# Moving a division by three key blocks, stores to another queue, and a normalisation into pairs, in a fused attention block

## The chip, the cores and the metric

The kernel runs on one core of one Trainium2 chip. The metric is the time of the core for one execution, in microseconds (us), as the median over several executions. A run is called slow when it is more than 1.5% above the fastest of its kernel.

## The reference, cut to what matters

```python
# x: (16, 512, 32, 32) float32; 8 groups, 4 heads of 128, n = 32 * 32 = 1024 positions
xn   = group_norm(x) * gamma + beta
q, k, v = split(einsum('oc,bchw->bohw', qkv_w, xn) + qkv_b)
attn = softmax(einsum('bhnd,bhmd->bhnm', q, k) * 128 ** -0.5)
out  = einsum('bhnm,bhmd->bhnd', attn, v)
return x + einsum('oc,bchw->bohw', proj_w, out) + proj_b
```

## The kernel before

It works through 16 batches of 4 heads of 8 key blocks. In each key block TensorE makes scores (s), ScalarE their exponential (p), VectorE adds p to a running sum (tot), and TensorE adds to the weighted sum (po). Between these, units of the big products are spread over the heads: q and k of heads 2 and 3 of the batch in head 0, the projection of the batch before in head 1, q and k of heads 0 and 1 of the next batch in head 2, v of the next batch in head 3. The big products use two levels of Strassen's scheme. Their weights, with the sums of weights worked out once, are kept in DRAM and loaded in groups into two buffers.

```python
wpool = ctx.enter_context(tc.tile_pool(name="w", bufs=2))

def group_weights(site, g, first):
    group = OUTER[g]                          # ((1, 5), (2, 6), (7, 4), (3,))
    w = wpool.tile([P, 2, 7, P], F32, tag="w", name=f"w_{site}_{g}")
    if not first:
        nc.sync.dma_start(w[:, : len(group)], store[site, g])     # 896 KB, or 448
        return w
    # ... first use: build the sums, keep them
```

So the third group of weights can be loaded only when the last product of the first group has read its buffer.

The inner sums of the activations are kept too, for the second pair of heads:

```python
def inner_sum(m):
    # ... a, c: the two terms of t1, t2, t3 or t4
    for i in range(n):
        nc.vector.tensor_sub(have[m][:, i, :], inner(i, a), inner(i, c))
    if sums == "keep":
        t = dpool.tile([P, n, Q], F32, tag=f"{m}_{g}", bufs=1, name=f"kept_{m}_{g}")
        inner_kept[b, g, m] = t
        nc.sync.dma_start(t, have[m][:, :n])
```

A head's output is divided by its sums of exponentials in the head that follows. The reciprocals take a round through DRAM:

```python
def denominators(b, h):
    # ... sums of tot over the partitions, reciprocal r
    nc.sync.dma_start(row.rearrange("o (c i) -> (o c) i", i=BLK), r)
    nc.sync.dma_start(rinv[b, h], row.to_broadcast((P, N)))

def divide(b, h):
    nc.vector.tensor_mul(os_[b, h], os_[b, h], rinv.pop((b, h)))

for s in range(steps + 1):
    # ... j: key block, units: what plan_head puts into this block
    for half in range(NH2):
        if s < steps:
            scores(s, half)
            if half == 0 and j == 2 and s > NB:
                divide(*where(s - NB)[:2])
        if s > 0:
            weighted_sum(s - 1, half)
        run(units[half * n : (half + 1) * n])
```

A scheduler orders each engine's queue when the kernel is built: it has a model of when inputs are there, and the place in the source decides only between candidates.

Names in the profile: w is a buffer of weights and kept its store in DRAM; xt is a sum of blocks of x, qk_t an inner sum (of parts of one block or block sum) and kept_t its copy in DRAM; qk_x and qk_y (the "y bank") hold TensorE's products for q and k until VectorE or ScalarE has emptied them, into qk_r among others; row and rinv are the reciprocals on their round through DRAM; vd and v are v on its way through DRAM.

## Time and profile before

| | before |
|---|---|
| time, median (range, runs) | 3326.03 us (3324.56 to 3336.82, 4) |
| span of the profiled run | 3336.0 us |
| TensorE busy | 3218.4 us (96%) |
| TensorE waits for the y bank behind the division | 69.2 us, 15 times |
| TensorE waits for weights (w<-kept) | 9.7 us, 17 times |

The lines behind these numbers stand in the prediction. In a line of waits the three numbers are the sum in us, how often, and the longest. In a line of the timeline they are the start and the length in us, then engine, source line, operation, output<-input; in brackets the idle time before it and what ended it. A line of the chain (the work that ended last) has start, length and transfer. A line of DMA issues ends with the size of one and the median us from issue to landing.

The profiled run is the slowest of the four, 11 us over their median, so some of its idle time may be that run's own.

One more table is worked out from the trace and not a view of the page. In this trace matmul instructions of 512 columns that follow each other without a break start 0.429 us apart, those of 256 columns 0.215 us. For each instruction I take the time from its start to the next one's start, less 0.4267 us for 512 columns and in proportion for fewer, and call the rest **idle time**: waits, what a lowered clock costs, and the 2 or 3 ns by which the amount taken off is too small (some 17 us). The work taken off is the same 3095 us in all kernels here, so a difference in span is a difference in idle time. A head begins with the last s of the head before, so that a gap just ahead of its own first s is its own; what follows the very last s is put in head 0:

| idle us, 15 batches | batch 0 | head 0 | head 1 | head 2 | head 3 | sum |
|---|---|---|---|---|---|---|
| before | 22.1 | 135.7 | 26.3 | 31.7 | 7.9 | 223.7 |

Head 0 holds the wait behind the division and the slower clock that goes with it.

### The profile page before, as it was taken

Reading aid. Unit: us, or ns where it says so; the run is one execution under the profiler, and the core shown is the slowest. Engines: PE = TensorE matmul, PEld = TensorE weight load, DVE = VectorE, ACT = ScalarE, POOL = GpSimd, SP = SyncE. Lnnn points to the kernel's source line nnn. Section 1 sums busy time; section 2 is a strip of 40 time slices with the busy share of each in tenths; the row PEclk is TensorE's granted clock in tenths of the full one; section 3 lists DMA queues with packets and bytes.
Section 4 is the critical chain, followed back from the end, with each engine's and each line's share of the span. In section 5 each row is a group of like instructions: output and inputs, shape, how many; then the busy total and the mean of one; then the engine's idle time right before and its main releaser. Section 6 shows DMA issues by size and latency. Waiting matters only on the chain.

```text
span 3336.0 us, 33513 instructions
## 1 busy us (share of the span) xinstructions
PE 3218.4 (96%) x10474; PEld 2187.3 (66%) x10474; DVE 2522.8 (76%) x4161; ACT 1440.8 (43%) x2709; POOL 387.4 (12%) x682
## 2 busy tenths in 40 slices
PE   8999999999999999999999999999999999999999
PEld 6566666666666666666666666666666666666664
DVE  7876868768687686877878677786777867778675
ACT  2534435344353443534435354353534535344342
POOL 0001021010211102011020100202002020020100
PEclk9999999999999999999999999999999999999999
DMA  6665564555645557454564645646456464564731
GB/s 222 213 207 176 171 212 142 183 173 180 204 160 177 169 171 217 154 185 154 186 203 157 196 146 178 207 152 201 149 172 216 152 203 151 168 206 161 221 127 45
DMA packets 227958, 589.27 MB, mean 177 GB/s; under 512 B 32960, under 2 KB 72384, under 8 KB 227776
## 3 DMA queue, kind: packets, MB, share of 16 engines
q1 hardware_dynamic: 176944, 427.63, 39.2%
q0 software_dynamic: 48960, 157.33, 15.0%
q10 hardware_dynamic: 1872, 2.11, 0.2%
q8 instruction: 86, 1.41, 0.2%
q14 instruction: 96, 0.79, 0.1%
HBM read 448.28 MB, written 138.67 MB: 176 GB/s over the span
## 4 chain that ended last, share of the span: by engine, by line
PE 66%; DVE 16%; DMA 10%; issue 6%; POOL 1%; ACT 0%; SPq 0%; POOLq 0%; DVEq 0%; ACTq 0%
PE po L796 18%; PE s L711 18%; PE qk_x L509 7%; PE qk_y L509 6%; PE v_x L509 5%; PE pp_x L509 4%; PE v_y L509 4%; PE pp_y L509 3%; DMA w<-kept 3%; DMA rinv<-row 2%; DMA row<-r 2%; DVE qk_t L494 2%; DVE tot L724 1%; DMA y<-in_x 1%; DVE vt L648 1%
## 5 line engine op out<-in xcount | busy, mean ns | idle before, releaser
L716 ACT ACTIVATE p<-s 128x512 f32<-128x512 f32 x1024 | 610.5, 596 | 1058.6 <-PE s L711 1051.8
L711 PE MATMUL s<-qk,qk 128*128 128x512 f32 x2048 | 1059.5, 599 | 2.7 <-ACT p L716 2.4
L796 PE MATMUL po<-p,v 128*128 128x512 f32 x2048 | 1059.6, 599 | 0.9 <-ACT o L803 0.9
L796 PEld LDWEIGHTS po<-p,v 128*128 128x128 f32 x2048 | 603.4, 303 | 335.5 <-issue 218.0
L724 DVE TENSOR_TENSOR tot<-tot,p 128x1024 f32<-128x1024 f32 x385 | 469.4, 1219 | 108.0 <-ACT p L716 105.0
L711 PEld LDWEIGHTS s<-qk,qk 128*128 128x128 f32 x2048 | 391.7, 192 | 98.4 <-issue 33.5
L509 PE MATMUL qk_x<-qk_t,w 128*128 128x256 f32 x1344 | 363.4, 387 | 8.4 <-ACT qk_u L420 6.5
L509 PEld LDWEIGHTS qk_x<-qk_t,w 128*128 128x128 f32 x1344 | 249.5, 192 | 183.9 <-issue 67.0
L528 DVE TENSOR_TENSOR qk_r<-qk_y,qk_u 128x512 f32<-128x512 f32 (+1 forms) x256 | 158.6, 619 | 159.6 <-ACT qk_u L420 134.6
L420 ACT COPY qk_u<-qk_x 128x512 f32<-128x512 f32 (+1 forms) x256 | 136.4, 533 | 261.1 <-PE qk_x L509 261.1
L659 POOL DMA_DIRECT2D vd<-vu x120 | 66.4, 553 | 1376.6 <-DVE vu L651 1350.9
L509 PE MATMUL qk_y<-qk_t,w 128*128 128x256 f32 x448 | 132.9, 412 | 69.1 <-DVE qk_r L528 68.9
L806 DVE TENSOR_TENSOR o<-o,rinv 128x1024 f32<-128x1024 f32 x63 | 77.1, 1225 | 144.2 <-DMA rinv<-row 143.7
L509 PE MATMUL pp_x<-pp_t,w_proj 128*128 128x256 f32 x630 | 173.3, 389 | 0.0
L509 PEld LDWEIGHTS v_x<-v_t,w_v 128*128 128x128 f32 x630 | 118.4, 190 | 79.1 <-issue 38.3
L509 PE MATMUL v_x<-v_t,w_v 128*128 128x256 f32 x630 | 166.6, 381 | 0.0
L528 DVE TENSOR_TENSOR v_r<-v_y,v_u 128x512 f32<-128x512 f32 (+1 forms) x120 | 74.6, 622 | 121.4 <-ACT v_u L420 113.6
L509 PEld LDWEIGHTS pp_x<-pp_t,w_proj 128*128 128x128 f32 x630 | 113.9, 190 | 63.7 <-issue 18.9
L664 POOL DMA_DIRECT2D v<-vd x240 | 139.8, 590 | 98.1 <-DMA vd<-vu 45.2
L509 PEld LDWEIGHTS qk_y<-qk_t,w 128*128 128x128 f32 x448 | 89.6, 204 | 92.1 <-DVE qk_r L528 74.5
L509 PE MATMUL qk_y<-x,w 128*128 128x256 f32 x512 | 145.7, 382 | 2.2 <-DVE x L272 2.1
L696 POOL DMA_DIRECT2D out_y<-y x120 | 66.2, 552 | 634.7 <-DVE y L695 631.6
(203 smaller groups left out, 4216.5 us busy)
## 6 DMA issues: line engine op xcount, KB each, us to landing
w<-kept SPq DMA_DIRECT2D x90, 896.0 KB, 5.9
kept_t<-qk_t SPq DMA_DIRECT2D x192, 256.0 KB, 2.2
qk_t<-kept_t SPq DMA_DIRECT2D x192, 256.0 KB, 4.7
v_t<-kept_t SPq DMA_DIRECT2D x180, 256.0 KB, 2.7
w_v<-kept_v SPq DMA_DIRECT2D x45, 896.0 KB, 4.7
w_proj<-kept_proj SPq DMA_DIRECT2D x45, 896.0 KB, 4.5
rinv<-row SPq DMA_DIRECT2D x63, 512.0 KB, 4.8
x<-in_x POOLq DMA_DIRECT2D x60, 512.0 KB, 5.7
```

Source lines behind the costliest of these rows:

```text
L420: nc.scalar.copy(t[n][:, :width], t["x"][:, :width])
L494: nc.vector.tensor_sub(have[m][:, i, :], inner(i, a), inner(i, c))
L509: nc.tensor.matmul(acc[:, ts(i, Q)], have["w"][:, i, SLOTS[an], :], inner(i, bn), start=(first and i == 0), stop=True, skip_group_check=True,)
L528: nc.vector.tensor_add(dst, view(a), view(c))
L659: nc.gpsimd.dma_start(rows[which][ts(h, P), :], u)
L664: nc.gpsimd.dma_start(vs[b, pair][ts(q, BLK), half].rearrange("m h (k i) j -> m (h k) (i j)", k=n), rows[which].rearrange("(k m) (q e) -> ...
L696: nc.gpsimd.dma_start(out[b, ts(o, P), ts(half, HALF)], t)
L711: nc.tensor.matmul(sc, ks[b, h][:, ts(j, P)], qs[b, h][:, ts(half, HALF)], start=True, stop=True)
L716: nc.scalar.activation(ps[s][:, ts(half, HALF)], sc, AF.Exp, scale=SCALE)
L724: nc.vector.tensor_add(tot[b, h][:, i], tot[b, h][:, i], ps[s][:, i])
L796: nc.tensor.matmul(po[b, h][:, i], v_block(b, h, j), ps[s][:, i], start=(j == 0), stop=(j == NB - 1),)
L806: nc.vector.tensor_mul(os_[b, h], os_[b, h], rinv.pop((b, h)))
```

## The change

Three intents: put the division of a head where its reciprocals have surely landed (sixth key block, and the block sums of o that read it behind it), take the stores of inner sums out of SyncE's queue, where they stand ahead of loads, and normalise x by pairs of chunks so that the first block sum can come sooner.

```diff
-    def x_sums(b):
-        xb[b] = halves([xs[b, c] for c in range(NCC)], "x")
-        sums_of_b(xb[b])
+    def x_sums(b, rows=(1, 2)):
+        if 1 in rows:
+            xb[b] = halves([xs[b, c] for c in range(NCC)], "x")
+        sums_of_b(xb[b], rows)
 ...
                     inner_kept[b, g, m] = t
-                    nc.sync.dma_start(t, have[m][:, :n])
+                    nc.gpsimd.dma_start(t, have[m][:, :n])
 ...
-                plan[3].append(lambda: o_blocks(b - 1))
-                plan[3].append(lambda: sums_of_b(ob[b - 1]))
+                plan[6].append(lambda: o_blocks(b - 1))
+                plan[6].append(lambda: sums_of_b(ob[b - 1]))
 ...
-                for half in range(NH2):
-                    plan[5 + half] += [
-                        lambda c=c, half=half: normalise(b + 1, c, half) for c in range(NCC)
+                for r in range(2):
+                    plan[5 + r] += [
+                        lambda c=c, half=half: normalise(b + 1, c, half)
+                        for c in range(KC * r, KC * r + KC) for half in range(NH2)
                     ]
-                plan[NB - 1].append(lambda: x_sums(b + 1))
+                    plan[6 + r].append(lambda r=r: x_sums(b + 1, (r + 1,)))
 ...   # last batch: one sum of o in block 5, not 4
-                if half == 0 and j == 2 and s > NB:
+                if half == 0 and j == 5 and s > NB:
                     divide(*where(s - NB)[:2])
```

More of the change, by code (lines that the diff above doesn't have):

```diff
@@ L974, in plan_head @@
                 plan[3].append(lambda: sums_of_b(ob[b], (1,)))
-                plan[4].append(lambda: sums_of_b(ob[b], (2,), (0,)))
+                plan[5].append(lambda: sums_of_b(ob[b], (2,), (0,)))
         elif h == 2:
```

## The prediction

> **What bounds the kernel now.** I read the busy line first, then TensorE's waits, then VectorE's waits, then one batch in order of time, and last the five heads of one batch by stage.
>
> ```profile
> PE 3218.4 (96%) x10474; PEld 2187.3 (66%) x10474; DVE 2522.8 (76%) x4161; ACT 1440.8 (43%) x2709; POOL 387.4 (12%) x682
> PE qk_y L509 <- DVE qk_r L528: 69.2, 15, 6.4
> PE qk_x L509 <- DMA w<-kept: 9.7, 17, 1.1
> PE qk_y L509 <- DVE x L272: 2.1, 4, 1.2
> DVE o L806 <- DMA rinv<-row: 143.7, 52, 8.4
> SPq L498 <- DVE qk_t L494: 443.8, 173, 11.2
> ```
>
> TensorE is the bound: 96% busy, and its only large wait is 69.2 us in 15 pieces, one in each batch but the first. Everything else it waits for is below 11 us over the whole run. VectorE waits 143.7 us for the spread reciprocals (rinv) ahead of the division of a head. SyncE's queue stands 443.8 us at the stores of inner sums, but nothing says yet that anybody needs what stands behind them.
>
> The chain, then VectorE, then TensorE around one of the 15 pieces:
>
> ```profile
> 465.94 4.66 DMA row<-r
> 470.62 7.47 DMA rinv<-row
> 478.11 1.23 DVE L806 TENSOR_TENSOR o<-o,rinv 128x1024 f32<-128x1024 f32 x1 [7.76 <-DMA rinv<-row]
> 481.31 0.68 DVE L528 TENSOR_TENSOR qk_r<-qk_y,qk_p 128x512 f32<-128x512 f32 x1
> 475.18 1.03 PE L509 MATMUL qk_x<-qk_t,w 128*128 128x256 f32 x4
> 482.05 2.08 PE L509 MATMUL qk_y<-qk_t,w 128*128 128x256 f32 x4 [5.84 <-DVE qk_r L528]
> ```
>
> [...]At 470.3 it has nothing to do but the division, which waits until two DMAs one behind the other have landed (4.66 + 7.47 us). Behind the division stand three subtractions of o (L272) and then the addition that empties the y bank. TensorE needs that bank and stands 5.84 us. So the 69.2 us are the division's wait, handed on through VectorE's queue, in the head that follows a batch (head 0 below, window 1088 to 1140).
>
> By stage (heads 1, 2, 3, then 0):
>
> ```profile
> 933.00:985.00 52.00, 51.90 (x169) 35.05 (x169) 44.59 (x79) 33.53 (x70) 7.61 (x13) 1.00 0.39 133
> 985.00:1037.00 52.00, 51.25 (x174) 35.73 (x173) 41.28 (x79) 19.75 (x36) 0.00 (x0) 1.00 0.53 179
> 1037.00:1088.00 51.00, 50.22 (x166) 34.75 (x165) 38.47 (x52) 19.73 (x35) 10.08 (x18) 1.00 0.67 202
> 1088.00:1140.00 52.00, 46.56 (x145) 31.19 (x145) 32.47 (x47) 17.16 (x32) 8.01 (x15) 0.93 0.64 194
> ```
>
> Columns are the length, busy us of PE, PEld, DVE, ACT and POOL, then granted clock, DMA share and GB/s. In three of four heads TensorE is idle for under 0.8 us. In head 0 it is idle 5.4 us, and only there is the clock below 1.00: 0.93, so 52 x 0.07 = 3.6 us of clock, part of it during the idling itself. Call it 2 us of slower matmuls per batch, an estimate.
>
> **What the Trainium skill says.** (1) "TensorE: Matmul & The Clock Gate", Part 1: after about one idle window of 3.4 us TensorE's clock falls to half and comes back after a busy one. The trace agrees: the only head with a wait over 3.4 us is the only one with a lower clock. So the 69.2 us carry about 15 x 2 = 30 us more with them; what is to be won by removing the wait is about 100 us, 3.0% of 3326. (2) "DMA: Bandwidth & Descriptors", Issuing engines are not separate DMA queues: issuing from several engines saves only the sequencer's time to initiate. So moving the stores helps only what stood behind them in SyncE's queue. (3) Same page, Specifications: the first byte comes after about 1 us on GpSimd's path, about 0.6 us on SyncE's. The trace agrees in size: a 256 KB store lands in a median 2.7 us from GpSimd (out_y) and 2.2 us from SyncE (kept_t), as the two lines below show. (4) "SBUF — State Buffer", the "DVE blocks DMA" trap: GpSimd can be kept from writing descriptors while VectorE runs an operation in a two-port mode. The trace shows no sign of it: GpSimd's issues take 552 to 590 ns on average beside a VectorE that is 62 to 86% busy.
>
> ```profile
> kept_t<-qk_t SPq DMA_DIRECT2D x192, 256.0 KB, 2.2
> out_y<-y POOLq DMA_DIRECT2D x120, 256.0 KB, 2.7
> ```
>
> **The change part by part.** The source diff is not the order in which instructions stand: a scheduler orders each engine's queue. I built the changed kernel and compared the queues with buffer numbers taken out.
>
> *Division in the sixth block, and the sums of o behind it.* As written, this would take the division from behind the wait: three blocks of some 6.5 us (52 / 8) later rinv has long landed, and the whole 100 us would go. But in the built order of VectorE the division after head 3 stands exactly where it stood: behind the first addition to tot of head 0, then the same three subtractions of o, then the additions into qk_r that empty the banks. This holds in every batch; VectorE's queue in head 0 has no difference at all. The scheduler starts an instruction when its own model says that the input is there, and the place in the source only breaks ties. The divisions after heads 0 and 2 stay as well. Only the one after head 1 moves, behind a few more instructions in head 2; there VectorE waited 0.82 us in the batch above and TensorE hardly at all. So this part is worth **0 us** of the 100.
>
> *256 stores to GpSimd.* Nothing is removed; 256 issues x 0.55 us = 141 us are added to GpSimd, 387 to some 528 us of 3326, or 9 us per batch, all in head 2, where GpSimd did 0.00 us. The order of GpSimd's other 695 instructions is unchanged. What it gives back is seen here:
>
> ```profile
> 992.37 1.03 PE L509 MATMUL qk_y<-x,w 128*128 128x256 f32 x4
> 991.07 3.17 SPq L498 DMA_DIRECT2D kept_t<-qk_t  x3
> 994.33 0.38 SPq L349 DMA_DIRECT2D w<-kept  x1
> 1001.00 1.10 PE L509 MATMUL qk_x<-xt,w 128*128 128x256 f32 x4 [0.72 <-DMA w<-kept]
> ```
>
> The weight buffer is free at 993.4 (992.37 + 1.03), the load goes out at 994.33 behind three stores: 0.9 us late, and TensorE waits 0.72 us. The stores gone, the load comes 0.9 us earlier. But in the changed order the matmul that needs it stands ahead of one s (two instructions, 0.86 us) rather than behind it, so it also wants the weights 0.86 us earlier. Net 0 to 9.7 us in all; I take **-3 us**. Against it: a store lands some 0.5 us later, and the next group's sum may overwrite its source only then. The tightest pair has about 0.7 us between landing and overwriting (two stores from 986.54 in 1.61 us, the second out at 987.8, 2.2 us to landing, next sum at 990.75). So at most a few tenths per batch: **+1 us**.
>
> *x normalised by pairs, first block sum moved.* Same eight activations, same eight subtractions. VectorE's queue has x_0 and x_1 subtracted twelve and some seventeen instructions earlier, at the second half of head 1, where it is saturated (44.59 of 52 us, and without a break from 974 to 985). This removes TensorE's wait for x (2.1 us here). The y additions come up to 1.3 us later, and the total ahead of the next inner sums is the same, so the end of head 1 stays VectorE's pace: **-2 us**, some given back at the y bank of pp.
>
> Sum: 0 - 3 + 1 - 2 = **-4 us**, so 3326 - 4 = 3322 us.
>
> **The rivals.** *A: the division is really late.* If the chip's order were the source's, the 69.2 us and the clock's 30 us go: about 3226 us. The profile speaks for the mechanism, the built order against its happening; the trace before follows the built order instruction by instruction (first tot, o, three L272, qk_r), so I trust it. *B: head 0's transfers become quicker or slower.* The wait is made by row<-r and rinv<-row; 15 pieces of 3.2 to 6.6 us vary with what else is in flight (0.64 share in head 0). All moved stores are in head 2, and SyncE's order in head 0 has no change, so rinv should go out the same 4.7 us after row. If it lands 1 us sooner: -15 us and a little clock, 3305 us; 1 us later: 3337 us. *C: GpSimd's stores hold up others:* v's own transfers from GpSimd in head 3, or sums waiting for a slow store in head 2. VectorE has 10.7 us to spare in head 2 and GpSimd nothing to do there, so at most 1 us per batch: 3340 us. *D: the boundary from head 1 to 2 gets better than I think,* all of 9.7 + 2.1 plus the small gaps there gone: 3310 us.
>
> **Range and chances.** Centre 3322. B, C and D are worth about 10 to 15 us each way, and the three runs before spread by 12 us, so 3300 to 3337 should hold it 8 in 10. Faster by over 2% means under 3259.5, which only A gives; slower by over 2% means over 3392.5, for which I see no mechanism of that size. Faster 0.04, same 0.95, slower 0.01.
>
> **What would show each step.** Right: TensorE still waits some 60 to 75 us for qk_r in 15 pieces; the division's wait for rinv is still 6 to 8 us in head 0, with the division right behind the first tot; head 0's clock is again about 0.93; SyncE's 443.8 us at the stores are gone; GpSimd's busy time is about 530 us; the wait for x is gone. Wrong: the 15 pieces vanish and the clock is 1.00 in head 0 (A), or they grow or shrink by 1 us each with rinv's time to landing (B), or VectorE waits for kept_t stores or v's transfers (C).

## The result, and the profile after

The changed kernel takes 3339.55 us (median of 4 runs, 3338.42 to 3345.45) against 3326.03 us: ratio 1.0037, 95% interval 1.0013 to 1.0061. A ratio is the mean time of one kernel's fast runs over that of the other's of the same rounds, so it is not quite the ratio of the medians quoted. Within 2% was right; 3339.55 lies 2.6 us above the range, and the sign was wrong: 13.5 us slower where 4 us faster was expected.

The changed kernel's busy line, TensorE's waits, and VectorE's wait at the division:

```profile
PE 3216.1 (96%) x10474; PEld 2183.1 (65%) x10474; DVE 2521.0 (75%) x4161; ACT 1437.4 (43%) x2709; POOL 525.6 (16%) x938
PE qk_y L510 <- DVE qk_r L529: 67.9, 15, 7.9
PE qk_x L510 <- DMA w<-kept: 18.4, 23, 2.1
PE qk_y L510 <- DVE qk_t L495: 4.6, 12, 1.3
DVE o L807 <- DMA rinv<-row: 129.0, 36, 9.8
```

The wait behind the division is where it was (69.2, now 67.9). The wait for weights has doubled, 9.7 to 18.4 us, and a wait for an inner sum (qk_t) of 4.6 us is new. In idle time:

| idle us, 15 batches | batch 0 | head 0 | head 1 | head 2 | head 3 | sum |
|---|---|---|---|---|---|---|
| before | 22.1 | 135.7 | 26.3 | 31.7 | 7.9 | 223.7 |
| after | 21.7 | 131.1 | 27.7 | **42.5** | 7.9 | 230.8 |

Head 2 lost 10.8 us. Head 0 won 4.6, less than two runs of one and the same kernel differ by there (132.1 in e14 and 125.6 in e18 below). So the loss is in head 2, which begins the next batch's q and k. The timeline of the changed kernel there, in the same batch as in the prediction:

```profile
984.08 0.67 PE L510 MATMUL qk_y<-qk_t,w 128*128 128x256 f32 x2 [0.25 <-DVE qk_t L495]
992.18 1.11 PE L510 MATMUL qk_y<-x,w 128*128 128x256 f32 x4
993.32 0.32 SPq L350 DMA_DIRECT2D w<-kept  x1
999.37 1.10 PE L510 MATMUL qk_x<-xt,w 128*128 128x256 f32 x4 [0.90 <-DMA w<-kept]
```

The stores have gone from SyncE's queue, and the load goes out as soon as its buffer is read out (992.18 + 1.11 = 993.29), where it was 0.9 us late before. Still the wait is 0.90 us, not 0.72. The issues of the changed kernel:

```profile
kept_t<-qk_t POOLq DMA_DIRECT2D x192, 256.0 KB, 2.9
w<-kept SPq DMA_DIRECT2D x90, 896.0 KB, 6.3
```

A store lands in 2.9 us from GpSimd, as expected; a load of weights takes 6.3 us in the median (5.9 before). Why the wait grew shows when the instances in head 2 are averaged over batches 1 to 14. (Batch 0, whose order differs, is left out; with it the gaps sum to 9.3 and 16.6 us, the figures that some expectations use. Batch 15 has no next batch.) "Work" is what TensorE has to do between the last read of the old weights and the first use of the new ones, "late" how long after that last read the load is issued (matmul ends are modelled; 0.03 means at once), "gap" the idle time ahead of the first use:

| head 2, mean of 14 batches, us | work | late | work less late | issue to use | gap | gaps, sum |
|---|---|---|---|---|---|---|
| before | 6.83 | 0.93 | 5.89 | 6.42 | 0.64 | 8.9 |
| after | 5.12 | 0.03 | 5.09 | 6.13 | 1.15 | 16.1 |

The load has 5.09 us instead of 5.89 until it is wanted. In the built TensorE queue two things moved: the first matmuls of the third group (qk_x<-xt) stand ahead of an s that they stood behind, and the last readers of the old weights (qk_y<-x) stand behind an s that they stood ahead of. Each takes 0.86 us out of the work that hides the load.

### The profile page after: what moved, and what is told of

It reads as the page before. It is cut to its first block, busy times and chain, and to the rows that moved or that the text cites. A ratio compares the mean times of both kernels' runs of the same rounds, so it can differ in the third digit from the quotient of the medians.

```text
span 3343.7 us, 33635 instructions
## 1 busy us (share of the span) xinstructions
PE 3216.1 (96%) x10474; PEld 2183.1 (65%) x10474; DVE 2521.0 (75%) x4161; ACT 1437.4 (43%) x2709; POOL 525.6 (16%) x938
## 3 DMA queue, kind: packets, MB, share of 16 engines
q8 instruction: 86, 1.41, 0.2%
## 4 chain that ended last, share of the span: by engine, by line
PE 57%; DVE 11%; issue 9%; DMA 9%; POOL 1%; ACT 0%; POOLq 0%; DVEq 0%; SPq 0%; ACTq 0%
PE po L797 16%; PE s L712 15%; PE qk_x L510 6%; PE qk_y L510 5%; PE v_x L510 4%; PE pp_x L510 3%; PE v_y L510 3%; PE pp_y L510 3%; DMA w<-kept 2%; DMA rinv<-row 2%; DMA y<-in_x 2%; DMA row<-r 2%; DVE xt L272 1%; DVE tot L725 1%; DVE vt L649 1%
## 5 line engine op out<-in xcount | busy, mean ns | idle before, releaser
L499 POOL DMA_DIRECT2D kept_t<-qk_t x256 | 138.2, 541 | 487.8 <-DVE qk_t L495 439.8
L807 DVE TENSOR_TENSOR o<-o,rinv 128x1024 f32<-128x1024 f32 x63 | 77.0, 1223 | 129.5 <-DMA rinv<-row 129.0
```

The lines of the kernel that those rows point to most:

```text
L499: nc.gpsimd.dma_start(t, have[m][:, :n])
```

## The experiments

Two theories at first. **Theory W** (weights): the loss is this order around the third load of weights. **Theory X** (pairs): it is the new order of x's normalisation and sums, which makes inner sums late. Later **theory D** (transfers) was added for head 0. All runs give the right result. Each is timed against the kernel before on the same chip, 5 rounds; the medians of before are 3330.18 (e1 to e4), 3330.7 (e5 to e8), 3333.95 (e9 to e12), 3330.23 (e13 to e16) and 3324.22 us (e17, e18). TensorE's stages by idle time, for most runs, are in one table at the end of this section.

### One part at a time: e1, e2, e3

e1 has the stores alone (`nc.sync` to `nc.gpsimd` in the line of kept inner sums), e2 x by pairs and the moved block sum alone, e3 all of the change but the stores.

> The kernel before with the 256 stores alone moved to GpSimd. Theory W (the loss is the wait for weights: the built order puts the first matmuls of the third group ahead of one s, while the load comes only 0.9 us sooner): TensorE's wait for w<-kept is 16 to 20 us as in the changed kernel (18.4) and not 9.7, and the time is 8 to 14 us over before, about 3336 us. Theory X (the loss is in the pairs of chunks, through the new wait of 4.6 us for inner sums): w<-kept may grow, but the time stays within 4 us of before.

> The kernel before with x normalised by pairs and its first block sum moved, nothing else. Theory W: within 3 us of before, about 3326 us; the wait of TensorE for x (2.1 us) is gone, a wait for inner sums (some 4 us) comes in its place. Theory X: 8 to 14 us slower than before.

> The changed kernel with its stores back in SyncE's queue. Theory W: the w<-kept wait is back to about 10 us and the time is back within 4 us of before, some 10 us under the changed kernel. Theory X: as slow as the changed kernel, about 3339 us.

Measured: e1 3349.61 us, ratio 1.0059 (1.0045 to 1.0072); e2 3343.67 us, 1.0044 (1.0026 to 1.0061); e3 3350.58 us, 1.0063 (1.0046 to 1.0081). Every part alone loses at least as much as the whole, and the parts don't add up. All three missed what theory W expected: e1 is 19 us slower, not 8 to 14, and by their times alone e2 and e3 speak for theory X, e1 against it. TensorE's waits in e1 and in e2:

```profile
PE qk_x L509 <- DMA w<-kept: 25.4, 16, 2.6
```

```profile
PE qk_x L510 <- DMA w<-kept: 24.2, 22, 1.8
PE qk_y L510 <- DVE qk_t L495: 9.5, 10, 3.0
```

But what theory W assumed of e2 and e3 was wrong in one point: the reordering does not come with the stores but with any of the edits. In the builds e1 and e2 both have qk_x<-xt ahead of the s. The scheduler decides anew at each edit. In e2 and e3 the last readers have moved as well, the work is 5.12 us and the gaps sum to 19.8 and 23.6 us, as the shorter cover says. In e1 only the first use moved: the work less late is 5.94, as before, just as the prediction reckoned for the stores, and yet its gaps sum to 25.0, because there the load takes 7.61 us from issue to use. In every batch of e1 a store starts about 0.8 us behind the load's issue, where in the kernel before SyncE's queue let none start in the first 4 us. That may be the reason: in e8 (below) one starts about 1.1 us behind it and the load takes 7.77 us, in e14 1.7 to 2.9 us behind and it takes 6.30. But no run moved that store alone, so it stays open.

### The division really moved: e4

The prediction said that the division stays put in the built queue. So in the kernel before it is tied behind the latest addition to tot in the sixth block, with a dependency that only orders VectorE's queue, for head 0 alone; the block sums of o go to `plan[6]` as in the change:

```diff
+                if half == 0 and j == 5 and s > NB and h == 0:
+                    with tc.issue_after(adds[0].ins):     # adds[0]: latest addition to tot
+                        divide(*where(s - NB)[:2])
```

> The kernel before, where the division after head 3 alone is made to stand behind the addition of the fifth block to tot, by an ordering edge (and the sums of o behind it). If the 69 us wait is the division's and carries the half clock with it, as the prediction says: TensorE's wait for qk_r in head 0 falls from 69.2 us to under 10, the clock in head 0 is 1.00, and the time falls by 80 to 105 us to 3221 to 3246 us. Rival: something else in head 0 (weights, inner sums, the y bank through ScalarE) takes the place of the wait: the time falls by less than 40 us and that wait shows in TensorE's list.

Measured: 3335.93 us, ratio 1.0013 (0.9999 to 1.0027). The waits of e4:

```profile
PE qk_x L509 <- DMA w<-kept: 76.9, 31, 5.8
PE qk_y L509 <- DVE qk_r L528: 0.3, 1, 0.3
```

The wait behind the division is gone, 69.2 to 0.3 us, and another of 76.9 us stands in its place. The load in the chain of e4 in head 0 and TensorE's timeline there, then the same stretch by stage (columns as in the prediction), then the issues of 473 to 485 us:

```profile
473.76 10.49 DMA w<-kept
484.29 2.07 PE L509 MATMUL qk_x<-xt,w 128*128 128x256 f32 x4 [4.54 <-DMA w<-kept]
```

```profile
473.80:484.30 10.50, 5.96 (x21) 3.90 (x19) 2.58 (x3) 2.37 (x4) 2.16 (x4) 0.95 1.03 306
```

```profile
x<-in_x POOLq DMA_DIRECT2D x2, 512.0 KB, 12.4
w<-kept SPq DMA_DIRECT2D x1, 896.0 KB, 10.5
y<-in_x POOLq DMA_DIRECT2D x3, 256.0 KB, 12.8
```

The load of the third group takes 10.49 us (10.8 on average over the 15 batches), not some 6, and TensorE has 5.97 us of work meanwhile. In the kernel before, the same load takes 10.9 us on average, but its first use comes only 12.8 us after its issue: it lay behind the wait for the y bank, two waits side by side, of which only one showed. The DMA engines are full (share 1.03): among others the next batch's x and the y residuals, wanted only in head 1, are loaded here.

### Taking the other transfers away: e5, e6

Hold the loads of x and y until late additions to tot in head 0:

```diff
                 dma = eng.dma_start(xs[b, c][:, i], x[b, ts(c, P), i])
                 if b > 0:
                     tc.keep_in_program_order(dma)
+                    hold(dma, b - 1, 5)        # behind the sixth block's addition, head 0
 ...
             dma = nc.gpsimd.dma_start(t, x[b, ts(o, P), ts(half, HALF)])     # residual
+            hold(dma, b + 1, 6)
```

e5 has e4's division, e6 only the hold. In the traces TensorE, VectorE, ScalarE and SyncE run in the order of e4 and of the kernel before; only GpSimd's differs.

> The kernel before with two edits: the division after head 3 behind the fifth block's addition to tot (as in e4_division_forced), and the loads of the next batch's x and of the y residuals held back until the sixth and seventh block's addition to tot in head 0. The queues of TensorE, VectorE, ScalarE and SyncE are those of e4 instruction for instruction; only GpSimd's order of loads differs. Theory D (transfers): the 76.9 us wait for w<-kept in e4 is there because 1 MB of x and 0.75 MB of y share the DMA engines with the 896 KB of weights; without them the weights land in some 6 us instead of 10.5, TensorE has 5.97 us of work meanwhile, so the wait falls to 5 to 25 us in all, the clock in head 0 comes back to 1.00, and the time falls 50 to 90 us below the kernel before: 3240 to 3280 us. Rival D2 (the SyncE queue's own inner sums delay the weights, or the held loads only move the wait to head 1): the wait for w<-kept stays above 50 us or stats and y are waited for in head 1, time 3310 to 3345 us.

> The kernel before with the same hold of x and y loads and the division left where it was, behind the first addition to tot. Theory D: rinv, 512 KB read behind row, also lands sooner when x and y are out of the way (some 5 us instead of 7.5), so the wait of TensorE for the y bank (69.2 us, 15 pieces) shrinks by 1.5 to 2.5 us a piece: 30 to 50 us left, time 3285 to 3310 us. Rival: rinv's time is made by row's latency and its own 128 copies, not by the other loads: 60 to 75 us left and the time within 6 us of the kernel before.

Measured: e5 3302.02 us, 0.9914 (0.9897 to 0.9930); e6 3303.6 us, 0.9921 (0.9903 to 0.9939). In e6 the wait for the y bank, and the chain that makes it in one batch:

```profile
PE qk_y L522 <- DVE qk_r L541: 45.7, 15, 4.1
465.10 2.87 DMA row<-r
467.99 7.42 DMA rinv<-row
```

In this batch row lands in 2.87 us instead of 4.66, and rinv takes as long as ever (7.42 against 7.47). On average over the 15 batches both land about 1 us sooner: row in 4.0 us instead of 4.9, rinv in 5.7 instead of 6.7. The wait falls from 69.2 to 45.7 us, and theory D holds for e6. e5 fell short of its expectation: w<-kept is still waited for 61.2 us, and in head 0 on average 9.26 us pass from issue to use. What is still in flight beside it is, in one batch, rinv (out at 464.76 in the timeline) and v's transfers (463.25 to 467.88), the load itself going out at 469.57. Not moving the division and moving it cost the same here.

### Putting the order back, and making the swap alone: e7, e9, e13, e14

e7 is the whole change with edges that have no semaphore and only order TensorE's queue: first use of the third group behind the next s traced, the next s behind the last readers of the first group. e9 is the kernel before with both edges the other way round. In the cut, order(later, earlier) stands for the call that adds such an edge:

```diff
+        while first_:      # in scores(): this s behind the last readers of group 0
+            order(one_s, first_.pop())
+        while third:       # the first matmuls of group 2 behind this s
+            order(third.pop(), one_s)
```

> The whole change, plus edges without a semaphore that put two pairs of TensorE instructions in head 2 back into the order of the kernel before: the last readers of the first weights buffer ahead of the s that had slipped ahead of them, and the first matmuls of the third group behind the s they had slipped ahead of. Theory W (the lost time is the order around the third weights load): PE work between last read and first use comes back from 4.8 to some 5.8 us, the wait for w<-kept falls from 18.4 to 3 to 8 us, and the time comes back by 8 to 14 us to 3324 to 3332 us. Rival (the loss sits elsewhere: the new waits for inner sums, 4.6 us, or smaller gaps all over): the time stays at 3336 to 3344 us although the wait falls.

> The kernel before, with nothing of the change but one thing that its build brought with it: edges without a semaphore put the last readers of the first weights buffer in head 2 behind the s that they stood ahead of, and the first matmuls of the third group ahead of the s that they stood behind (another po slips between, so the work that covers the load shrinks by one s, 0.86 us, a batch). Theory W: TensorE's wait for w<-kept grows by 10 to 14 us (9.7 to some 22), idle time in head 2 from 31.7 to some 44 us, and the time by the same, ratio 1.003 to 1.0045. Rival (the swap is harmless, the loss of the change comes from its moved work): ratio within 0.001 of 1.

Measured: e7 3350.75 us, 1.0061 (1.0043 to 1.0078); e9 3341.99 us, 1.0033 (1.0015 to 1.0052). At face value e7 is against theory W and e9 for it, but neither is a clean test. The idle time in batch 0 rose to 30.9 and 29.1 us (22.1 before): the edges also acted in batch 0. In e7 one wait there is 8.39 us:

```profile
168.66 2.05 PE L512 MATMUL qk_x<-x,w 128*128 128x256 f32 x4 [8.39 <-DMA w<-kept]
```

e13 and e14 repeat e9 and e7 with the edges only from the third batch's q and k on (`b > 1`).

> As e9, the edges only from the third batch's q and k on, so that batch 0 keeps its order and its stall of 7 us is gone. Theory W: head 2's idle time grows from 31.7 to 38 to 44 us and the ratio is 1.002 to 1.0035. Rival (e9's loss was the stall in batch 0; its profile had head 2 at 32.0): ratio within 0.0015 of 1, head 2 at 30 to 34 us.

> As e7, the edges only from the third batch's q and k on. Theory W: with the wait for w<-kept at 5.7 us in head 2 (e7) and no stall in batch 0 the ratio falls from the change's 1.0037 to 1.000 to 1.002. Rival (the loss has other sources: inner sums that come late because two of the block sums and the first tot stand elsewhere, and the spread of the runs): 1.003 to 1.0045.

Measured: e14 3333.18 us, 1.0005 (0.9986 to 1.0024): no loss clear of the noise is left. e13 3333.22 us, 1.0009 (0.9990 to 1.0028): nor does the swap in the kernel before cost any. The table of covers says why. In e13 the readers come later by one s, but by then the stores ahead of the load in SyncE's queue are out and it goes out almost at once, so work less late is 5.90 us, as before. By these figures it is not an order as such that loses, but 5.1 us of cover; no run gave the kernel before that little cover by itself.

As the intervals of e14 and of the change overlap, both ran once more, on one chip:

> The changed kernel itself, timed beside e18 on one chip. Expected 1.003 to 1.005 against the kernel before, idle time of head 2 at 40 to 45 us. Under 1.0015 would mean that the loss first measured was chance.

> The kernel of e14 again, beside e17. Theory W: 0.002 to 0.004 under e17 and within 0.0015 of the kernel before, head 2 at 32 to 35 us idle. Rival (e14's return was chance or the chip): within 0.0015 of e17.

Measured: e17, the change itself, 3341.21 us, 1.0045 (1.0027 to 1.0064); e18 3329.02 us, 1.0007 (0.9986 to 1.0029). The wait for weights in e17, and the waits of e18:

```profile
PE qk_x L510 <- DMA w<-kept: 16.7, 22, 2.9
```

```profile
PE qk_y L512 <- DVE qk_r L535: 67.1, 15, 6.8
PE qk_x L512 <- DMA w<-kept: 6.9, 13, 1.3
PE qk_y L512 <- DVE qk_t L497: 4.5, 11, 1.2
```

| head 2, mean of 14 batches, us | work less late | issue to use | gap | idle in head 2, sum of 15 |
|---|---|---|---|---|
| before | 5.89 | 6.42 | 0.64 | 31.7 |
| e13 swap in the kernel before | 5.90 | 6.37 | 0.55 | 29.9 |
| e14 change, order back | 5.94 | 6.30 | 0.47 | 33.4 |
| e18 the same again | 5.94 | 6.17 | 0.34 | 30.0 |
| after | 5.09 | 6.13 | 1.15 | 42.5 |
| e17 the same again | 5.09 | 6.07 | 1.09 | 42.8 |
| e2 pairs only | 5.07 | 6.38 | 1.41 | 53.8 |
| e1 stores only | 5.94 | 7.61 | 1.78 | 46.8 |

e17 and e18 differ by 12.2 us in the median, and every run of e17 is above every run of e18. Head 2's idle time differs by 12.8 us, 10.4 of it (15.2 less 4.8) at the first use of the third group. In the traces the two differ, per batch, in the places of two s on TensorE, one addition to tot and one exponential, all in head 2. So this order loses most of the change's time; the 4.8 us by which e18's median still is above the kernel before are within the noise. The new wait for inner sums stays in e18 (4.5 us), so theory X is not what loses the time in the whole change; in e2, where that wait is 9.5 us, it may add to the loss.

### Splitting the load: e10, e11, e12, e15

If only the last byte of the weights is late, the first products need not wait for it. They read the first two of seven slots:

```diff
-            nc.sync.dma_start(w[:, : len(group)], store[site, g])
+            for slots in (slice(0, 2), slice(2, 7)):
+                nc.sync.dma_start(
+                    w[:, : len(group), slots], store[site, g][:, :, slots]
+                )
```

e10 has this and e4's division, e11 also the hold of e5, e12 is the whole change with the split, e15 the kernel before with the split.

> As e4 (division after head 3 behind the fifth block's addition), and each load of weights in two pieces, the two slots that the first two products read (256 KB) ahead of the five others (640 KB). Theory: what replaced the wait for the y bank in e4 is only that the weights' last byte lands late, so with the first slots 256 KB long the wait of 76.9 us falls below 20 us, head 0's idle time falls from 138.5 to some 50 us, and the 100 us of the prediction appear: 3225 to 3260 us, ratio 0.97 to 0.98. Rival: DMA engines are so full there (share 1.02) that the first piece lands late too, or the second piece is then waited for by the third product: wait above 45 us, time 3290 to 3335 us.

> e10 and the hold of the x and y loads of e5. If e10's rival is right and the transfers are what counts, this one is faster than e10 by 20 to 40 us; if the split alone already takes the wait away, the hold adds under 10 us. Expected 3220 to 3250 us.

> The whole change with the weights' loads in two pieces and nothing else. Theory W: head 2's wait for w<-kept (16.6 us in the change) falls below 4 us, so idle time in head 2 falls from 42.5 to under 32 us and the time comes to 8 to 16 us below the change, ratio 0.999 to 1.002 against the kernel before; the wait for the y bank behind the division (67.9 us) stays. Rival (the loss is the inner sums' waits and small gaps): ratio stays at 1.003 or more.

> The kernel before with each load of weights in two pieces, nothing of the change. By the idle time: head 2 has 9.3 us of gaps at the first matmul of the third group, so 7 to 10 us are to be won: ratio 0.997 to 0.998, head 2 at 21 to 24 us idle. Then the change with the split load (1.0002) is still 0.002 to 0.003 behind its own control and the weights' wait is only about half of the change's loss. If instead the ratio is 0.999 to 1.0, the wait for weights is the whole of it.

Measured: e10 3317.15 us, 0.9956 (0.9941 to 0.9972); e11 **3237.51 us, 0.9719** (0.9701 to 0.9736); e12 3331.95 us, 1.0002 (0.9981 to 1.0022); e15 3324.55 us, 0.9977 (0.9959 to 0.9995). The waits for weights in e10 and in e11:

```profile
PE qk_x L512 <- DMA w<-kept: 56.0, 15, 4.9
```

```profile
PE qk_x L525 <- DMA w<-kept: 14.1, 13, 2.3
```

e10 missed: in full queues the first piece is late too (10.64 us from its issue to its use in head 0, with a mean gap of 3.89 us), and the rival's 3290 to 3335 holds. With the hold it takes 6.88 us, and head 0's idle time falls from 135.7 to 45.4 us. e10 and e11 differ in GpSimd's order alone. The mean granted clock of the whole run is 0.998, against 0.987 in the kernel before. So some 100 us were there, 3333.95 less 3237.51 is 96, but it took three edits: each of the three waits (y bank, weights, full engines) hid the next. Of the 99.8 us less idle time (table below) 90.3 are in head 0; 10.4 are in head 2, where the split alone wins as much (12.0 in e15). e11 is faster than both kernels and is the one to keep.

e12 and e15: the split wins 8 us in the kernel before and about 13 in the change. By e15's expectation the 0.0025 left between them would mean that the wait for weights is only about half of the change's loss. That is less than their intervals can tell apart, and e17 against e18 says more. But e12 does have 6.1 us more idle time in head 2 than e15, under 1 us of it at the first use of the third group, so the rest of the new order may cost a few us too. The split is not a pure test of the wait either: in the trace of e15 TensorE's order differs from the kernel before, the first use standing ahead of one s.

### The change as its text reads: e8, e16

In e8 the whole change has each division tied behind the last addition to tot ahead of it in the source, in all heads, and the hold; e16 has the split load too.

> The whole change as its text reads: each division tied behind the latest addition to tot that stands ahead of it in the source (so it really comes in the sixth block), with the stores in GpSimd's queue, x by pairs, and x and y loads held as in e5. Theory D: as e5, plus the 10 to 15 us that the order of head 2 costs: 3250 to 3292 us, wait for w<-kept 20 to 40 us, wait for the y bank behind the division below 5 us. Rival D2: 3320 us or more.

> e8 (whole change, divisions tied to the sixth block, x and y loads held) with the weights' loads in two pieces. If e8 lost because the weights' last byte was waited for (99.9 us), this one comes near e11's 3237: 3238 to 3262 us, ratio 0.972 to 0.979, slower than e11 by the waits e8 shows in head 3 (18.2 us idle instead of 7.9) and in head 2. Rival: other waits that the change brings take the place again, 3290 us or more.

Measured: e8 3354.77 us, 1.0075 (1.0057 to 1.0094), with a wait for weights of 99.9 us; e16 3284.71 us, 0.9857 (0.9835 to 0.9878). Both missed. e16 is 47 us slower than e11, and this is mostly in head 0 (81.9 us idle against 45.4) and head 3 (17.7 against 7.9). In its timeline, in one batch, the last eight transfers of v are issued from 470.88 to 475.51 and rinv at 472.69, right beside the load of weights at 474.85, while in e11 they are out at 459.04 to 463.67 and 460.53, well before the load at 465.53. That the divisions in other heads push v's work back is a likely cause; no run tied them one by one.

| idle us, 15 batches | batch 0 | head 0 | head 1 | head 2 | head 3 | sum |
|---|---|---|---|---|---|---|
| before | 22.1 | 135.7 | 26.3 | 31.7 | 7.9 | 223.7 |
| e1 stores only | 23.3 | 134.6 | 27.5 | 46.8 | 7.8 | 239.9 |
| e4 division | 23.4 | 138.5 | 24.8 | 28.8 | 8.3 | 223.8 |
| e5 division, hold | 21.3 | 103.0 | 26.2 | 33.6 | 7.8 | 191.9 |
| e6 hold | 22.9 | 96.7 | 26.3 | 33.4 | 8.0 | 187.3 |
| e7 change, order back | 30.9 | 132.4 | 27.0 | 37.5 | 8.4 | 236.3 |
| e8 change, divisions, hold | 22.9 | 129.5 | 28.1 | 53.4 | 18.2 | 252.1 |
| e10 division, split | 22.3 | 128.0 | 25.7 | 20.3 | 7.8 | 204.1 |
| e11 division, split, hold | 22.7 | 45.4 | 26.6 | 21.3 | 7.9 | 123.9 |
| e12 change, split | 25.1 | 127.8 | 25.4 | 25.8 | 7.8 | 212.0 |
| e15 split | 21.6 | 135.6 | 26.3 | 19.7 | 7.8 | 210.9 |
| e16 the same, split | 25.1 | 81.9 | 25.7 | 25.4 | 17.7 | 175.9 |
| e17 change again | 22.7 | 129.8 | 25.4 | 42.8 | 7.8 | 228.5 |
| e18 change, order back | 23.0 | 125.6 | 27.4 | 30.0 | 7.8 | 213.8 |

## Why the prediction was wrong, point by point

- **The division is worth 0 us**: right. It stays in its place in the built queue and the wait is 67.9 us, in 15 pieces. Of the signs, 60 to 75 us of wait (67.9), no stores in SyncE's queue, GpSimd near 530 us (525.6) and no wait for x came true. Signs of this kind did not test the step that failed. Two readings are a little off: the pieces of the wait are 14 of 3.0 to 6.4 us and one of 0.3, not 15 of 3.2 to 6.6, and of the 256 stores 240 start in head 2, not all.
- **The stores, -3 us**: this is the step that failed. It said: "But in the changed order the matmul that needs it stands ahead of one s (two instructions, 0.86 us) rather than behind it, so it also wants the weights 0.86 us earlier. Net 0 to 9.7 us in all". It compared the first use of the new weights with the time of issue, and left out that the last readers of the old weights had moved as well, to behind an s. The cover shrank by 6.83 - 5.12 = 1.71 us, twice the 0.86, while the load was issued 0.90 us sooner after the last read, as predicted: 0.8 us less for the load in each batch, where the prediction had about 0. The wait grew by 8.7 us instead of shrinking by 3. Putting these instructions back gives the loss back (e14, and e17 against e18: 12.2 us). e1 shows a second gap in this step: with the stores alone the cover is what the prediction reckoned, and the time is still lost, because the load takes 7.61 us instead of 6.42; why stays open.
- **A store lands later, +1 us**: right in size for the landing (2.9 us). The wait looked for came, VectorE's for a store ahead of an inner sum (3.1 us in 5 pieces, none before). Another came too, TensorE's for an inner sum (4.6 us), and this one is not the stores': e2, without them, has 9.5 us of it. e18 still has it without being slower.
- **x by pairs, -2 us**: the wait for x (2.1 us) did go. What e2 adds that the prediction did not see is that this part alone changes TensorE's order as well, the last readers included, and costs 1.0044.
- **Rival A, about 100 us if the division were really late**: the size was nearly right (96 us in e11, some 90 of it in head 0), the condition was not enough. Some 31 of the 90 are matmuls that run over 0.05 us longer than they should with no wait behind them (39.6 us of such time before, 8.8 in e11), where the prediction estimated 30 us for slower matmuls. The record of the clock agrees with the prediction's reading of "TensorE: Matmul & The Clock Gate", Part 1: before, head 0 has 15 stretches at half clock of 3.4 or 6.8 us, in e11 two. e4 shows that with the division late the time does not change: the third load of weights had been hidden behind the wait. The prediction's profile lines held the hint: 0.64 DMA share in head 0, and rinv at 7.47 us.
- **Range**: it had 15 us above the centre, for rinv and for GpSimd's stores holding up others. That rival C names 3340 us, next to the 3339.55 measured, is luck: of its signs only VectorE's 3.1 us came. The direction in which the order of TensorE's own queue could move was not among the rivals.

## What to carry to other kernels

Where a scheduler orders the queues, look at both ends of every load's cover in the built order, the last reader of the old buffer and the first user of the new one, before counting what an earlier issue wins; any edit may move either. Before crediting a wait with its length, look for a second transfer that lands inside it: taking away the division's wait alone won nothing, with the loads that fill the engines moved away and the weights split it won 96 us. And check the start-up batch when an edge is added for the steady state: 8 us there turned a test round.

## What the Trainium skill lacked or had wrong

- "DMA: Bandwidth & Descriptors", Issuing engines are not separate DMA queues, says that issuing from several engines saves only the sequencer's time. No run here speaks against it: with the stores in GpSimd's queue the load of weights went out 0.90 us sooner, and e18, with TensorE's order put back, is no faster than the kernel before (1.0007). What it lacks is what landing costs when the engines are full: the same 896 KB load took 6.3 us in the median of the changed kernel, and 10.49 us at a DMA share of 1.03 in e4; row, 4 KB, took 4.9 us on average in head 0 and 4.0 us with other loads held (e6).
- "Perfetto Trace Analysis", DMA Optimizations, has it that splitting DMAs may let some start sooner, but no page says to split a load by the order in which its parts are read. Two pieces (256 KB, read first, and 640 KB) won 0.2% alone (e15), and took e5's 0.9914 to 0.9719 (e11); with full engines (e10) the first piece was still used only 10.64 us after its issue.
- No page has it that the built order of a queue can change around an edit that does not touch its engine: moving stores from SyncE to GpSimd (e1) put the first use of the third group ahead of one s in TensorE's order, in each batch from 1 to 14.
